# First routed layer: a part of the token tiles gathered in quarters and transposed on VectorE

## The chip, the core and the metric

The kernel runs on one core of one Trainium2 chip. The metric is the device time of one execution in microseconds; the median of several runs counts. The engines are named as in the profile: PE is TensorE (PEld its weight loads), DVE VectorE, ACT ScalarE, POOL GpSimd, SP the SyncE queue that issues plain DMAs. The granted TensorE clock averaged 0.948 of full speed in the profiled execution.

## The reference

Two layers of a gated cross-attention block with a mixture of experts behind each attention, on x of 4 x 512 tokens with 512 features, in float32. The part that matters here is the mixture of experts of the first layer:

```python
h = layernorm(x).reshape(2048, 512)
scores = sqrt(softplus(h @ gate_w.T))                 # 32 experts
_, topk_idx = top_k(scores + bias, 6)
topk_w = 1.5 * scores[topk_idx] / sum(scores[topk_idx])
pos = running count of each expert's tokens;  valid = pos < 192
xb[e, pos] = h of the token                           # 32 experts x 192 slots x 512
g = xb[e] @ w_gate[e].T ; u = xb[e] @ w_up[e].T       # 256 wide
yb[e] = (silu(g) * u) @ w_down[e].T
routed = sum over the six picks of topk_w * yb[e, pos]
x = x + tanh(g_ffn[0]) * (routed + shared expert of h)
```

Ahead of it stands the first attention (each token picks two of 64 context rows), behind it the second attention (causal, 16 heads) and a second mixture (8 experts, two picks, 352 wide, and a shared expert).

## The kernel before

**Stages.** From 0 to about 150 us the kernel runs the first attention, the norm, the gate of the first mixture and a part of its shared expert. `turn2` writes each normed tile `h` (128 tokens by 512) to `h_dram` through SP (L471) and transposes it for the gate. `gate2` computes the picks and weights; it writes the weights of each token for all 32 experts behind the token's row in `h_dram` (L552, rows of 512 + 32 floats). The running counts of the experts' tokens go to `cnt_dram` (L670). Then comes the routed loop (156 to 455 us), in which 32 experts with 192 slots each are 48 tiles of 128 slots: tiles 3q and 3q+2 hold the first and last 128 slots of the experts 2q and 2q+1, and tile 3q+1 holds the remaining 64 of both, which is called a split tile here (`parts0`).

**The routed loop** has these steps, each for one tile i:

- `find0` (L761, POOL): an indirect DMA that fetches 128 floats of counts for each slot into `found`; `count0` (L774 to L779, DVE) compares and sums them, which gives the token of each slot, `get2`. Both work on groups of four tiles (`FIND`).
- `get0` (L783, POOL): an indirect DMA that gathers the 128 tokens' rows of 544 floats into `xb`.
- `in0`: four 128x128 transposes on PE into PSUM (`ptb`, L256) and an eviction by ACT (L257) into `xbT`.
- `up0`: four matmuls of 128x512 per expert part (L801), Silu on ACT (L806), the weighted product on DVE (L808, one instruction for each expert part), which reads the slot's weight out of `xb`.
- `turn0`: two transposes (`ptj`, L817) and an eviction (L819).
- `down0`: two matmuls of 128x512 per expert part (L826), and DVE copies the result to `y` (L831), which SP stores to `y_dram` (L886).
- `weights0`: SP loads an expert's up weights (1 MB, L558) and down weights (512 KB, L559) into one of three buffers.

The order is written by hand: PE, DVE, POOL and SP carry out the instructions in program order; ahead of the loop, the order on POOL and SP is a planner's. The loop's order is

```python
for i in range(NT2):
    up0(i + 1); in0(i + 2)
    if i % 4 == 0: count0(i // 4 + 2)      # and find0 of the next group begins
    get0(i + 4); next(find, None)          # one find in each iteration
    y = down0(i)
    weights0(i + 3)
    nc.sync.dma_start(out=y_dram[...], in_=y)
    turn0(i + 1)
```

Tiles of the tag `row` (nine buffers) hold `xb`, `y` and, earlier, `h`. PSUM tags have two buffers each.

**The second mixture** (its routed tiles run from 693 us on) already has tiles that are transposed on DVE: `pair_rows4` gathers rows, SP copies them quarter by quarter so that partition 32r + s holds quarter r of the tokens, and `in4_blocks` runs one DVE instruction (L1425) that transposes every 32x32 block. The features then lie in another order over the partitions, and the weights of that layer are laid out to match (`by_32` on the host).

Of the kernel before, what the change touches and what calls it, by code (L numbers as in the profile page):

```python
# [59 lines left out]

GROUPS = [[TB * b + g for b in range(B)] for g in range(TB)]
EARLY = 2
PLACE = {t: (g, j) for g, ts in enumerate(GROUPS) for j, t in enumerate(ts)}
# [13 lines left out]
def flamingo_gated(  # L77
# [423 lines left out]
    def gate2(p):  # L501
# [47 lines left out]
        )  # L549
        hd = h_dram.rearrange("(k j p) d -> p k j d", j=TB, p=P)  # L550
        for a in range(2):
            nc.sync.dma_start(out=hd[:, :, 2 * p + a, D:], in_=wts[:, :, a, :])  # L552


# [198 lines left out]

    FIND = [range(0, 2), range(2, 4)] + [range(i, i + 4) for i in range(4, NT2, 4)]
    found = {}
# [15 lines left out]
    def count0(k):  # L771

        c, n, f = slice(FIND[k][0], FIND[k][-1] + 1), len(FIND[k]), found.pop(k)
        V.tensor_tensor(f[:, :n], f[:, :n], slots2[:, c, None].to_broadcast([P, n, P]), ALU.is_le)  # L774
        tok = tok2[:, c]
        ct = sm.tile([P, 4], F32, name=f"ct{k}", tag="ct")
        V.tensor_reduce(ct[:, :n], f[:, :n], AX.X, ALU.add)
        V.tensor_tensor(tok, tok, ct[:, :n], ALU.add)
        V.tensor_scalar(get2[:, c], tok, float(T - 1), None, ALU.min)  # L779

    def get0(i):
        rows0[i] = work.tile([P, D + E0], F32, name=f"xb{i}", tag="row", bufs=NROW)
        G.indirect_dma_start(  # L783
# [8 lines left out]
    def in0(i):  # L792
        xbTs[i] = work.tile([P, DC, P], F32, name=f"xbT{i}", tag="xnT", bufs=3)
        transposed(xbTs[i], rows0[i], f"ptb{i}")

    def up0(i):
        xbT, xb = xbTs.pop(i), rows0.pop(i)
        gu = ps.tile([P, 2 * I0], F32, name=f"gu{i}", tag="g")
        for c in range(DC):
# [7 lines left out]
        for p_, e in parts0(i):  # L807
            V.scalar_tensor_tensor(  # L808
                sg[p_, :I0], gu[p_, I0:], xb[p_, D + e : D + e + 1], sg[p_, :I0], ALU.mult, ALU.mult
            )  # L810
# [55 lines left out]
    in0(1)  # L866
    turn0(0)
    for i in range(NT2):
        if i + 1 < NT2:
            up0(i + 1)  # L870
        if i + 2 < NT2:
            in0(i + 2)
        k = i // 4 + 2
        if i % 4 == 0 and k < len(FIND):
            count0(k)
            find = find0(k + 1) if k + 1 < len(FIND) else iter(())
        if i + 4 < NT2:
            get0(i + 4)
        next(find, None)
        y = down0(i)  # L880
# [514 lines left out]
    xrs, xrTs, xqs, sgs, its = {}, {}, {}, {}, {}  # L1395
    B4 = P // 32

    def rows4(i):
# [124 lines left out]
def _host_layout(i):  # L1523
# [35 lines left out]
    for j in range(2):  # L1559
# [17 lines left out]
        "bias0": c(np.asarray(i["L0_ffn_bias"])),  # L1577
        "wgu0": k_major(beside(i["L0_ffn_w_gate"], i["L0_ffn_w_up"])),
        "wd0": k_major(t(i["L0_ffn_w_down"])),
# [35 lines left out]
```

## Time and profile before

| | us |
|---|---|
| median of 3 runs | 1103.65 (1103.22 to 1107.76) |
| the profiled execution | 1109.61 |
| its span, first to last instruction | 1107.9 |
| PE busy in the span | 1007.1 (91%) |
| DVE busy | 466.1 (42%) |
| POOL busy | 376.3 (34%) |
| ACT busy | 210.9 (19%) |
| DMA, both queues | 52.7% of 16 engines' span |

The profile is of one execution. A row of its groups gives line, engine, operation, output and inputs, shapes and count, then busy time and mean length of one, then the idle time of the engine just before these instructions and what ended it. "L256" is the helper that does all PE transposes, so the tile names (`ptb`, `pth`, ...) tell them apart. A busy PE need not be PE at its peak, as matmuls overlap: the distance between starts tells what one costs. In the timeline, consecutive instructions of one group are merged into one line with their count.

### The profile page before, as it was taken

Reading aid. Unit: us, or ns where it says so; the run is one execution under the profiler, and the core shown is the slowest. Engines: PE = TensorE matmul, PEld = TensorE weight load, DVE = VectorE, ACT = ScalarE, POOL = GpSimd, SP = SyncE. Lnnn points to the kernel's source line nnn. Section 1 sums busy time; section 2 is a strip of 40 time slices with the busy share of each in tenths; the row PEclk is TensorE's granted clock in tenths of the full one; section 3 lists DMA queues with packets and bytes.
Section 4 is the critical chain, followed back from the end, with each engine's and each line's share of the span. In section 5 each row is a group of like instructions: output and inputs, shape, how many; then the busy total and the mean of one; then the engine's idle time right before and its main releaser. Section 6 shows DMA issues by size and latency. Waiting matters only on the chain. (4 is left out here: it accounts for less than half of the span.)

```text
span 1107.9 us, 11070 instructions
## 1 busy us (share of the span) xinstructions
PE 1007.1 (91%) x3334; PEld 492.9 (44%) x3334; DVE 466.1 (42%) x1244; ACT 210.9 (19%) x461; POOL 376.3 (34%) x413
## 2 busy tenths in 40 slices
PE   5479889999999999969779896999999998999998
PEld 2134444444444444424434443655555555544443
DVE  5989946322222232357787443122222222218111
ACT  1144121222222222123343200211111111110000
POOL 2001142234332222276552562445545454310000
PEclk7679999999999999989969798999999999999999
DMA  8522047688788787765563107527453744438111
GB/s 320 234 76 77 11 125 238 222 275 283 257 294 287 253 288 248 252 204 172 145 206 115 48 5 207 184 74 238 133 163 107 248 115 145 135 117 313 38 38 38
DMA packets 88477, 191.94 MB, mean 173 GB/s; under 512 B 24638, under 2 KB 42078, under 8 KB 82016
## 3 DMA queue, kind: packets, MB, share of 16 engines
q1 hardware_dynamic: 59808, 114.59, 29.3%
q0 software_dynamic: 28608, 76.63, 23.4%
q8 instruction: 27, 0.44, 0.2%
q14 instruction: 34, 0.28, 0.1%
HBM read 206.16 MB, written 35.57 MB: 218 GB/s over the span
## 5 line engine op out<-in xcount | busy, mean ns | idle before, releaser
L801 PE MATMUL gu<-wbuf,xbT 128*128 128x512 f32 (+1 forms) x512 | 174.0, 596 | 1.7 <-ACT xbT L257 0.8
L967 POOL DMA_INDIRECT yk<-y_dram,rows_of x76 | 84.1, 1107 | 89.1 <-DMA kb<-in_kblk_dram 34.7
L783 POOL DMA_INDIRECT xb<-h_dram,get x48 | 48.1, 1002 | 165.5 <-issue 97.3
L1436 PE MATMUL pgr<-wbuf,xrT 128*128 128x352 f32 x288 | 93.2, 467 | 7.4 <-DMA wbuf<-in_wgu_dram,wrow 6.7
L1456 PE MATMUL por<-wbuf,itr 128*128 128x512 f32 (+1 forms) x216 | 98.7, 592 | 0.0
L801 PEld LDWEIGHTS gu<-wbuf,xbT 128*128 128x128 f32 (+1 forms) x512 | 63.1, 163 | 78.7 <-issue 77.3
L808 DVE SCALAR_TENSOR_TENSOR sgb<-gu,xb,sgb 128x256 f32<-128x256 f32 (+1 forms) x64 | 30.9, 483 | 157.6 <-ACT sgb L806 131.8
L1439 DVE SCALAR_TENSOR_TENSOR sgr<-pur,slots,sgr 128x352 f32<-128x352 f32 x36 | 21.0, 584 | 170.0 <-PE pur L1436 105.1
L826 PE MATMUL pob<-wbuf,itb 128*128 128x512 f32 (+1 forms) x256 | 91.2, 599 | 0.0
L1436 PE MATMUL pur<-wbuf,xrT 128*128 128x352 f32 x288 | 91.1, 459 | 0.0
L1227 PE MATMUL pg<-lnT,wbuf 128*128 128x512 f32 (+1 forms) x224 | 85.3, 560 | 0.1
L1459 POOL DMA_INDIRECT y_dram<-yr,put x36 | 36.9, 1025 | 126.5 <-DVE yr L1458 113.6
L1227 PE MATMUL pu<-lnT,wbuf 128*128 128x512 f32 (+1 forms) x224 | 79.5, 531 | 0.0
L1436 PEld LDWEIGHTS pur<-wbuf,xrT 128*128 128x128 f32 x288 | 54.7, 190 | 30.5
L1436 PEld LDWEIGHTS pgr<-wbuf,xrT 128*128 128x128 f32 x288 | 52.7, 193 | 32.1 <-issue 4.5
L1243 PE MATMUL po<-wbuf,it 128*128 128x512 f32 x128 | 61.2, 612 | 3.0 <-DVE x L1253 3.0
L1456 PEld LDWEIGHTS por<-wbuf,itr 128*128 128x128 f32 (+1 forms) x216 | 41.0, 190 | 41.9 <-issue 34.9
L761 POOL DMA_INDIRECT found<-cnt_dram,look x48 | 48.7, 1014 | 25.9 <-issue 14.0
L1227 PEld LDWEIGHTS pg<-lnT,wbuf 128*128 128x128 f32 (+1 forms) x224 | 35.6, 183 | 43.8 <-issue 42.0
L1227 PEld LDWEIGHTS pu<-lnT,wbuf 128*128 128x128 f32 (+1 forms) x224 | 35.0, 175 | 40.8 <-issue 38.1
L831 DVE COPY y<-pob 128x512 f32<-128x512 f32 x48 | 33.2, 692 | 45.3 <-PE pob L826 32.0
L1458 DVE TENSOR_TENSOR yr<-por,half_db 128x512 f32<-128x512 f32 x36 | 24.9, 692 | 57.5 <-PE por L1456 51.2
(398 smaller groups left out, 1279.2 us busy)
## 6 DMA issues: line engine op xcount, KB each, us to landing
wbuf<-in_wgu_dram SPq DMA_DIRECT2D x32, 1024.0 KB
wbuf<-in_wd_dram SPq DMA_DIRECT2D x32, 512.0 KB
y_dram<-y SPq DMA_DIRECT2D x48, 256.0 KB
q<-rp SPq DMA_DIRECT2D x256, 32.0 KB
y<-y_dram SPq DMA_DIRECT2D x32, 256.0 KB
lnT<-in_xT_dram SPq DMA_DIRECT2D x4, 1024.0 KB
x<-in_x_dram SPq DMA_DIRECT2D x16, 256.0 KB
h_dram<-h SPq DMA_DIRECT2D x16, 256.0 KB
```

The costliest lines, as they stand in the source:

```text
L761: G.indirect_dma_start(out=found[k][:, j, :], out_offset=None, in_=cnt_dram[:, :], in_offset=bass.IndirectOffsetOnAxis(ap=look2[:, i : i + ...
L783: G.indirect_dma_start(out=rows0[i], out_offset=None, in_=h_dram[:, :], in_offset=bass.IndirectOffsetOnAxis(ap=get2[:, i : i + 1], axis=0) ...
L801: PE.matmul(gu[p_, :], lhsT=xbT[:, c, p_], rhs=weights[e][0][:, c, :], start=(c == 0), stop=(c == DC - 1),)
L808: V.scalar_tensor_tensor(sg[p_, :I0], gu[p_, I0:], xb[p_, D + e : D + e + 1], sg[p_, :I0], ALU.mult, ALU.mult)
L826: PE.matmul(po[p_, :], lhsT=it[:, ic, p_], rhs=weights[e][1][:, ic, :], start=(ic == 0), stop=(ic == I0 // P - 1),)
L831: V.tensor_copy(y, po)
L967: G.indirect_dma_start(out=yk, out_offset=None, in_=y_dram[:, :], in_offset=bass.IndirectOffsetOnAxis(ap=rows_of[:, t, k : k + 1], axis=0) ...
L1227: PE.matmul(p_[m, :n], lhsT=wgu[:, a, c, i], rhs=lnT[g][:, c, k], start=(c == 0), stop=(c == DC - 1))
L1243: PE.matmul(po, lhsT=it[:, ic, k * P : (k + 1) * P], rhs=wd[:, ic, :] if ic < 2 else wd2, start=(ic == 0), stop=(ic == 2),)
L1436: PE.matmul(p_, lhsT=xbT[:, c, :], rhs=wgu[:, a, c, :], start=(c == 0), stop=(c == DC - 1))
L1456: PE.matmul(po, lhsT=it[:ni, ic, :], rhs=wd[:ni, ic, :], start=(ic == 0), stop=(ic == 2))
L1459: d = G.indirect_dma_start(out=y4_dram[:, :], out_offset=bass.IndirectOffsetOnAxis(ap=put4[:, i : i + 1], axis=0), in_=yr, in_offset=None, ...
```

## The change

Of the 48 tiles, 18 are handled in another way: those of every second pair of experts from the sixth on (tiles 15 to 17, 21 to 23, ..., 45 to 47; `hops`). For these

- `get0` issues five indirect DMAs instead of one: four gather 128 rows of 128 floats (quarters of a token's row, out of a second copy of h, `hq_dram`), so that partition 32r + s of block a holds quarter r of the token of slot 32a + s; the fifth gathers the 32 weights of each slot's token from `w_dram`;
- `in0` is one DVE transpose of 32x32 blocks from SBUF to SBUF, with no PE transposes and no eviction by ACT;
- the row numbers of the quarters come from one small matmul (`quarters0`: 128x128 `same_b` by 12 columns, PE) and a conversion on DVE; `count0` has two small instructions more;
- the up and gate weights of those experts are laid out on the host with `by_32`.

Finds and counts go by groups of three tiles from tile 12 on, in an order written out by tables; the gathers of the 18 tiles are issued five iterations ahead, the others four as before. In the stage ahead of the loop, `turn2` stores each h a second time (`hq_dram`), `gate2` stores the weights a second time (`w_dram`), and POOL makes the constants `quarter`, `in_quarter` and `same_b`.

```diff
+HOP = 15
...
+    hq_dram = dram.tile([T, D], F32, name="hq_dram")
+    w_dram = dram.tile([T, E0], F32, name="w_dram")
...
+    B4 = P // 32
+    quarter = sm12.tile([P, 1], F32, name="quarter")
+    in_quarter = sm12.tile([P, B4], F32, name="in_quarter")
+    same_b = sm12.tile([P, P], F32, name="same_b")
+    G.memset(in_quarter, 0.0)
+    G.memset(same_b, 0.0)
+    for a in range(B4):
+        G.memset(quarter[32 * a : 32 * a + 32, :], float(a))
+        G.memset(in_quarter[32 * a : 32 * a + 32, a : a + 1], 1.0)
+        for r in range(B4):
+            G.tensor_tensor(
+                same_b[:, 32 * r : 32 * r + 32], same_b[:, 32 * r : 32 * r + 32], ident[:, 32 * a : 32 * a + 32], ALU.add
+            )
+    spread = sm12.tile([P, 3 * B4], F32, name="spread")
...
             nc.sync.dma_start(out=h_dram[t * P : (t + 1) * P, :D], in_=h)
+            nc.sync.dma_start(out=hq_dram[t * P : (t + 1) * P, :], in_=h)
...
-        hd = h_dram.rearrange("(k j p) d -> p k j d", j=TB, p=P)
+        hd, wd_ = [d.rearrange("(k j p) d -> p k j d", j=TB, p=P) for d in (h_dram, w_dram)]
         for a in range(2):
             nc.sync.dma_start(out=hd[:, :, 2 * p + a, D:], in_=wts[:, :, a, :])
+            nc.sync.dma_start(out=wd_[:, :, 2 * p + a, :], in_=wts[:, :, a, :])
...
-    FIND = [range(0, 2), range(2, 4)] + [range(i, i + 4) for i in range(4, NT2, 4)]
+    FIND = [range(0, 2), range(2, 4), range(4, 8), range(8, 12)]
+    for i in range(HOP, NT2, 6):
+        FIND += [range(i - 3, i), range(i, i + 3)]
+    hops = [i for t in range(HOP, NT2, 6) for i in range(t, t + 3)]
+    wcols, quarter_idx = {}, {}
...
         V.tensor_scalar(get2[:, c], tok, float(T - 1), None, ALU.min)
+        if FIND[k][0] in hops:
+            V.tensor_scalar(tok, tok, float(T - 1), None, ALU.min)
+            V.tensor_tensor(
+                spread[:, : 4 * n].rearrange("p (j a) -> p j a", a=B4),
+                tok[:, :, None].to_broadcast([P, n, B4]), in_quarter[:, None, :].to_broadcast([P, n, B4]), ALU.mult,
+            )
+
+    def quarters0(k):
+
+        n = len(FIND[k])
+        pi = ps.tile([P, 4 * n], F32, name=f"pi{k}", tag="u")
+        PE.matmul(pi, lhsT=same_b, rhs=spread[:, : 4 * n], start=True, stop=True)
+        idx = sm12.tile([P, 4 * n], I32, name=f"qi{k}", tag="qi", bufs=2)
+        V.tensor_scalar(idx, pi, 4.0, quarter, ALU.mult, ALU.add)
+        wc = sm12.tile([P, n, E0], F32, name=f"wc{k}", tag="wc", bufs=2)
+        for j, i in enumerate(FIND[k]):
+            quarter_idx[i], wcols[i] = idx[:, 4 * j : 4 * j + 4], wc[:, j, :]
 
     def get0(i):
+        if i in hops:
+            rows0[i] = work.tile([P, B4, P], F32, name=f"xq{i}", tag="row", bufs=NROW)
+            hq = hq_dram.rearrange("t (r d) -> (t r) d", d=P)
+            for dst, src, idx, n in [
+                *((rows0[i][:, a, :], hq, quarter_idx[i][:, a : a + 1], 4 * T) for a in range(B4)),
+                (wcols[i], w_dram, get2[:, i : i + 1], T),
+            ]:
+                G.indirect_dma_start(
+                    out=dst, out_offset=None, in_=src[:, :],
+                    in_offset=bass.IndirectOffsetOnAxis(ap=idx, axis=0), bounds_check=n - 1, oob_is_err=False,
+                )
+            return
...
         xbTs[i] = work.tile([P, DC, P], F32, name=f"xbT{i}", tag="xnT", bufs=3)
+        if i in hops:
+            V.transpose(
+                out=xbTs[i].rearrange("p c (a t) -> p a c t", a=B4),
+                in_=rows0[i].rearrange("p a (c t) -> p a c t", t=32),
+            )
+            return
         transposed(xbTs[i], rows0[i], f"ptb{i}")
...
+    counts_at, gets_at, finds_at = {0: 2, 4: 3}, {}, {i: [3] for i in range(4)}
+    for i in range(4, NT2):
+        gets_at.setdefault(i - (5 if i in hops else 4), []).append(i)
+    for k, ts in enumerate(FIND[4:], 4):
+        counts_at[ts[0] - (6 if k % 2 else 5)] = k
+        for j in range(3):
+            at = 4 + j // 2 if k == 4 else ts[0] - 9 + j
+            finds_at.setdefault(at, []).append(k)
+    finds = {k: find0(k) for k in range(3, len(FIND))}
     for i in range(NT2):
...
-        k = i // 4 + 2
-        if i % 4 == 0 and k < len(FIND):
-            count0(k)
-            find = find0(k + 1) if k + 1 < len(FIND) else iter(())
-        if i + 4 < NT2:
-            get0(i + 4)
-        next(find, None)
+        if i - 1 in counts_at and FIND[counts_at[i - 1]][0] in hops:
+            quarters0(counts_at[i - 1])
+        if i in counts_at:
+            count0(counts_at[i])
+        for j in gets_at.get(i, ()):
+            get0(j)
+        for k in finds_at.get(i, ()):
+            next(finds[k])
```

More of the change, by code (lines that the diff above doesn't have):

```diff
@@ L797, in up0 @@
         xbT, xb = xbTs.pop(i), rows0.pop(i)
+        wc = wcols.pop(i) if i in hops else xb[:, D:]
         gu = ps.tile([P, 2 * I0], F32, name=f"gu{i}", tag="g")
@@ L808, in up0 @@
             V.scalar_tensor_tensor(
-                sg[p_, :I0], gu[p_, I0:], xb[p_, D + e : D + e + 1], sg[p_, :I0], ALU.mult, ALU.mult
+                sg[p_, :I0], gu[p_, I0:], wc[p_, e : e + 1], sg[p_, :I0], ALU.mult, ALU.mult
             )
@@ L1395, in flamingo_gated @@
     xrs, xrTs, xqs, sgs, its = {}, {}, {}, {}, {}
-    B4 = P // 32
     def rows4(i):
@@ L1577, in _host_layout @@
         "bias0": c(np.asarray(i["L0_ffn_bias"])),
-        "wgu0": k_major(beside(i["L0_ffn_w_gate"], i["L0_ffn_w_up"])),
+        "wgu0": np.stack([
+            (by_32 if q >= HOP // 3 and q % 2 == HOP // 3 % 2 else k_major)(beside(i["L0_ffn_w_gate"][e], i["L0_ffn_w_up"][e]))
+            for q, e in ((e // 2, e) for e in range(E0))
+        ]),
         "wd0": k_major(t(i["L0_ffn_w_down"])),
```

## The prediction

> **What bounds the kernel now.** I read the page's groups first, to see which engine is without idle time in the first layer's routed loop (48 tiles, 156 to 455 us), then the windows of the loop, and then its timeline for two tiles.
>
> ```profile
> L801 PE MATMUL gu<-wbuf,xbT 128*128 128x512 f32 (+1 forms) x512 | 174.0, 596 | 1.7 <-ACT xbT L257 0.8
> L783 POOL DMA_INDIRECT xb<-h_dram,get x48 | 48.1, 1002 | 165.5 <-issue 97.3
> ```
> TensorE waits 1.7 us in all before the 512 up matmuls, while GpSimd sat idle 165.5 us before its 48 gathers.
>
> ```profile
> 300.00:318.00 18.00, 18.00 (x68) 7.82 (x67) 4.68 (x8) 4.03 (x9) 4.20 (x5) 1.00 0.90 307
> 318.00:336.00 18.00, 18.00 (x68) 7.83 (x67) 5.05 (x11) 4.03 (x9) 7.98 (x8) 1.00 0.87 288
> ```
> Columns: length, then busy time of PE, PEld, DVE, ACT and POOL, clock, DMA share, GB/s. TensorE is busy 18.00 of 18 us at full clock: the loop runs at TensorE's pace. The second thing to see is 0.90 and 0.87: the DMA engines are nearly full. From 246 to 444 us the windows average 0.80.
>
> ```profile
> L256 PE MATMUL ptb<-ident,xb 128*128 128x128 f32 x192 | 29.8, 278 | 2.3 <-DMA xb<-h_dram,get 2.3
> ...
> L1425 DVE STREAM_TRANSPOSE xrT<-q 128x512 f32<-128x512 f32 x32 | 22.4, 701 | 0.0
> ```
> The first row is what the change takes away from 18 tiles, the second, from the second layer, is what it puts there: an identical instruction.
>
> ```profile
> 291.67 0.60 PE L256 MATMUL ptb<-ident,xb 128*128 128x128 f32 x4
> ...
> 292.11 1.88 PE L826 MATMUL pob<-wbuf,itb 128*128 128x512 f32 x4
> ...
> 295.30 1.00 POOL L783 DMA_INDIRECT xb<-h_dram,get  x1 [15.14 <-issue]
> ...
> 296.60 1.00 POOL L761 DMA_INDIRECT found<-cnt_dram,look  x1 [0.30 <-issue]
> ...
> 297.73 0.66 PE L256 MATMUL ptb<-ident,xb 128*128 128x128 f32 x4
> ...
> 298.22 1.88 PE L826 MATMUL pob<-wbuf,itb 128*128 128x512 f32 x4
> 298.29 0.98 DVE L808 SCALAR_TENSOR_TENSOR sgb<-gu,xb,sgb 64x256 f32<-64x256 f32 x2 [3.14 <-ACT sgb L806]
> ...
> 299.94 0.38 PE L817 MATMUL ptj<-ident,sgb 128*128 128x128 f32 x2
> ...
> 300.16 3.60 PE L801 MATMUL gu<-wbuf,xbT 128*128 128x512 f32 x8
> ...
> 300.86 0.33 SPq L886 DMA_DIRECT2D y_dram<-y  x1
> ...
> 301.28 0.50 SPq L558 DMA_DIRECT2D wbuf<-in_wgu_dram  x1
> ...
> 312.17 3.65 PE L801 MATMUL gu<-wbuf,xbT 128*64 128x512 f32 x16
> ```
> Matmul starts give the pace: a tile takes 297.73 - 291.67 = 6.06 us (6.02 over many). The four transposes hold TensorE from 291.67 to 292.11, 0.44 us, and in their neighbours 0.49 and 0.53. GpSimd issues one indirect DMA per 1.30 us. A split tile's weights (L558, 301.28) are issued behind the store of a finished tile (300.86); by the trace's packet records they land at 309.7, and their tile starts at 312.17: 2.4 us of slack. Two later ones have 3.9 and 3.3.
>
> The way into the loop:
>
> ```profile
> 136.00 0.91 SPq L552 DMA_DIRECT2D h_dram<-wts  x2
> ...
> 137.01 0.46 SPq L558 DMA_DIRECT2D wbuf<-in_wgu_dram  x1
> ...
> 140.79 0.36 SPq L670 DMA_DIRECT2D cnt_dram<-counts  x1
> ...
> 144.10 1.71 POOL L761 DMA_INDIRECT found<-cnt_dram,look  x1 [11.60 <-DVE chain L704]
> ```
> ```profile
> 154.64 0.66 PE L256 MATMUL ptb<-ident,xb 128*128 128x128 f32 x4 [2.32 <-DMA xb<-h_dram,get]
> ```
> These stores run in one row: packets of wts 136.90 to 138.49, of wgu to 141.77, of the counts to 142.84, and only then can the finds start. TensorE waits for the end of this chain, 2.32 us.
>
> **The change, part by part.**
>
> *Removed from TensorE:* 18 of 48 tiles lose their four transposes: 18 x 0.49 (mean of 0.44, 0.49, 0.53) = 8.8 us, all on the path. The Trainium skill (TensorE: Matmul & The Clock Gate, Part 4) gives about 275 ns for one transpose in a kernel's context, and the row above says 278; by that 72 of them would be 20 us. But 278 ns is one's length, pipeline included, and the next work starts 0.44 to 0.53 us after four. I take the starts: 8.8. The 18 ScalarE evictions (0.59 each) bring nothing; ScalarE is busy 4 of 18 us.
>
> *Added to TensorE:* six index matmuls (`same_b` by 12 columns). Nearest is the second layer's 128x8 one, L1028: four of them are 8 records in 1.87 us, first starts 0.22 apart, two records each, so 0.44. Six: 2.6 us; if the loads hide, half: 1.3.
>
> *VectorE's transposes:* 18 x 0.70 us. VectorE has room (5 of 18 us busy), but it is in order: the transpose of tile i+2 stands behind the weighting of tile i+1 (L808) and must end before up0(i+2). For a whole tile L808 ends about 1.05 us after up0; plus 0.70 that is just in time for the 1.94 to 2.15 us of down and turn. Behind a split tile there are two L808 (0.98): 298.29 + 0.98 + 0.70 = 299.97, while TensorE without transposes would be ready at 297.73 + 1.72 + 0.22 = 299.67. With semaphores 0.35 us, six times: 2.1 us (0 to 3.5). That is where the cover by ptb goes. Two small instructions per count and one for the index (0.17 to 0.2 each) lie in VectorE's idle time.
>
> *GpSimd:* a converted tile issues five gathers for one. Six tiles then take 6 finds + 3 + 15 = 24 DMAs x 1.30 = 31.2 us of about 35; before it was 15.6 of 36. Not the bound on average, but no longer ahead. Let S be the start of the iteration five before a converted group. Index matmul and conversion end near S + 4.7, so the first quarter starts at S + 4.9. Behind it the other group's third find is number 11 (S + 19.2) and the next converted group's third find number 20 (S + 30.9). A DMA lands 3.1 to 8.4 us after issue in the loop (packet records; 5.7 in the mean). The counts that need them come up on VectorE about 5.2 us into the third and 5.7 us into the fifth iteration after S, with 5.85 us each at S + 22.8 and S + 35.0. Finds land at 25 and 36.6: VectorE waits some 2 us at each, with `y`'s copy, the next L808 and transpose queued behind it. What it costs TensorE through late L808s and index matmuls: most is absorbed in two `o` buffers; I take 0.4 us for each of five pairs, 2.0 us (0 to 8).
>
> *SP and the weights:* the count at S + 35 delays the copy and store of tile b, the first of its group; directly behind that store in SP's queue is wgu of the next split tile. A 2 us wait plus the count's 1.7 us puts the store some 3 to 4 us late against 2.4 to 3.9 us of slack, from which the faster tiles take another 1. Excess about 0.6 us in five pairs: 3.0 us (0 to 10).
>
> *DMA load:* a converted tile moves 256 + 16 KB instead of 272. The old gather is 64 packets of 207 ns. For four gathers of 128 rows of 512 B the nearest row is the find, same shape: 16 packets each, median 182 but mean 490 ns. So 11.6 to 31.4 us of packet time against 13.2: per engine -0.1 to +1.1 us per tile, plus about 0.1 for the 128 B rows. Finds read few, shared rows; spread rows should be near the low end. I take nothing and keep +1.1 for the range.
>
> *A port rule against the change:* the Trainium skill (SBUF — State Buffer, the box on DVE blocking a SWDGE DMA) says that GpSimd cannot write descriptors during a two-port VectorE instruction. Were the transpose one, 0.70 us of lockout per tile would be 2.1 of GpSimd's 4 us of slack per pair. In the second layer GpSimd's gathers (L1262) keep 1.007 us where L1425 runs, so I count none.
>
> *Before the loop:* two more stores of 64 KB in 128 B rows (w_dram) stand in SP's queue ahead of wgu and the counts. The same bytes took 136.90 to 138.49, so the finds start 1.6 us later, and TensorE's 2.32 us wait grows by that: 1.6 us (0 if SP's planner puts the counts ahead). The 16 hq stores (4 MB) fall at 62 to 105 us, DMA share 0.2: hidden; without that cover about 14 us. GpSimd's 26 small set-up instructions (0.1 to 0.3 each) lie in its idle time from 7.6 to 88 us. By the reordered weights of six expert pairs no byte changes.
>
> **Sum:** -8.8 + 2.6 + 2.1 + 2.0 + 3.0 + 1.6 = +2.5 us, on the profiled execution's 1109.61 (span 1107.9, 1.7 around it) about 1112. That execution lies 6 us over the median of the runs; the difference carried over gives 1103.65 + 2.5 = 1106. Against this kernel a measurement can tell about 0.5%, 5.5 us, from no change.
>
> **The rivals.**
>
> 1. *Break-even*, as summed: 1106, own range 1099 to 1109. Chance 0.47.
>
> 2. *Late weights.* DMA share is already 0.9, and wgu waits in SP behind a store behind a count. It decides once the count's wait passes about 2.4 us, or packets near 490 ns stretch a 4 us weight load by a tenth. Then both split tiles of a pair are late, 11 times by 1.2 us: +13 instead of +3, in all +12.5: 1116. Against: TensorE shows no weight wait today. Chance 0.27.
>
> 3. *GpSimd becomes the bound.* At a pitch of 1.5 instead of 1.30 us, 24 DMAs are 36 us, over the 35 of six tiles; the chain find, count, index, gather then sets the pace, about 1.5 us per pair beyond the sum: +10, 1114; with longer landings +20. Against: every kind of indirect DMA here takes 1.0 to 1.1 us. Chance 0.18.
>
> 4. *All waits absorbed.* Index matmul at 1.3, transpose stall 1.0, no late count or weight: -8.8 + 1.3 + 1.0 + 0.8 = -5.7: 1098. For: VectorE has two thirds free. Against: finds' landing times as measured. Chance 0.08.
>
> **Numbers.** Predicted 1106. From 1098 (rival 4) to 1122 (rivals 2 and 3 without their far ends). Faster 0.08, same 0.47, slower 0.27 + 0.18 = 0.45.
>
> **What would show it.** Right: ptb at 120 instead of 192; 18 STREAM_TRANSPOSE of 0.70; GpSimd near nine tenths in converted stretches; VectorE waiting on DMA before L774's instruction inside the loop, none today; up0 waiting 0.3 us on transposes behind split tiles; first find 1.6 us later. Wrong: idle before the up matmuls above 12 us and released by wbuf (rival 2); a GpSimd pitch above 1.4 or VectorE's transposes waiting on quarters (rival 3); six tiles in under 35.2 us (rival 4).

## The result, and the profile after

In the first measurement the changed kernel took 1164.91 us (median of 4 runs, 1160.02 to 1167.72) against 1105.70 for the kernel before (4 runs, 1103.22 to 1108.89): a ratio of 1.053, 95% interval 1.0486 to 1.0574. Two later sets of runs of the same two kernels, on chips that the results number 4 and 8, gave this:

| set | kernel before | changed kernel | ratio, 95% interval |
|---|---|---|---|
| first | 1105.70 | 1164.91 | 1.053, 1.0486 to 1.0574 |
| chip 4 | 1101.80 | 1108.52 | 1.0053, 1.0033 to 1.0074 |
| chip 8 | 1109.98 | 1161.82 | 1.0491, 1.0442 to 1.0539 |

(The chip of the first set is not on record.) The ratios are over fast runs and differ a little from those of the medians; front_only, in the table of the experiments, had two slow runs in twenty, which its median counts. The same program costs 0.5% on one chip and 5% on another. So there are two questions: what the change costs wherever it runs, and what adds some 50 us on some chips. The first set's profile shows the second. Its groups, for the whole program:

```profile
L864 PE MATMUL gu<-wbuf,xbT 128*128 128x512 f32 (+1 forms) x512 | 190.9, 632 | 16.0 <-issue 13.0
L839 POOL DMA_INDIRECT xb<-h_dram,get x30 | 30.1, 1004 | 75.0 <-issue 36.5
L833 POOL DMA_INDIRECT xq<-hq_dram,qi x72 | 71.7, 996 | 76.3 <-DVE qi L820 56.2
```
These answer to the up matmuls and the row gathers shown of before. TensorE now waits 16.0 us ahead of the up matmuls, 13.0 of it for "issue", that is for nothing that the profile shows. GpSimd's gathers are still 1.00 us each, and it still has idle time: 75.0 and 76.3 us.

The two windows of the loop (columns as before: length, busy PE, PEld, DVE, ACT, POOL, clock, DMA share, GB/s):

```profile
300.00:318.00 18.00, 13.31 (x28) 5.15 (x29) 3.81 (x9) 1.51 (x4) 9.03 (x10) 0.83 0.51 161
318.00:336.00 18.00, 17.77 (x65) 7.66 (x64) 7.37 (x17) 3.19 (x8) 6.48 (x7) 1.00 0.77 268
```
In the first window TensorE is busy 13.31 of 18 us at a clock of 0.83, and the DMA engines fell from 0.90 to 0.51, so they are not what is short. From the first transpose of the loop to its last down matmul it is 352.0 us; it was 298.5 (156.93 to 508.9, and 154.64 to 453.2, in the traces).

The clock is a part of the loss. In the loop of before it is granted in full throughout; here it is halved in eight stretches, 43.5 us in all, and each of them begins during a wait of TensorE's of over 1 us or within 2 us after one. The stretch inside the first window, and the time behind it:

```profile
299.40:302.80 3.40, 3.02 (x4) 1.47 (x5) 0.00 (x0) 0.33 (x1) 2.65 (x3) 0.50 0.31 85
302.80:306.00 3.20, 2.18 (x5) 0.62 (x4) 0.69 (x1) 0.00 (x0) 2.43 (x3) 1.00 0.26 86
```
A 128x512 matmul that starts in such a stretch lasts 1.03 us in the mean, the others 0.60. Over the loop TensorE is idle 41.1 us where it was 2.7, and busy 310.8 us where it was 295.9, although 72 transposes are gone. The waits come first and the slower clock comes on top.

The timeline tells what TensorE waits for. From the up matmuls of tile 19 to the silu of tile 20, while GpSimd gathers the quarters of tiles 21 to 23:

```profile
290.67 3.65 PE L864 MATMUL gu<-wbuf,xbT 128*64 128x512 f32 x16
291.28 1.00 POOL L833 DMA_INDIRECT xq<-hq_dram,qi  x1 [0.30 <-issue]
292.58 0.99 POOL L833 DMA_INDIRECT xq<-hq_dram,qi  x1 [0.30 <-issue]
...
294.26 0.65 PE L275 MATMUL ptb<-ident,xb 128*128 128x128 f32 x4
294.75 1.88 PE L889 MATMUL pob<-wbuf,itb 128*128 128x512 f32 x4
...
296.31 0.38 ACT L869 ACTIVATE sgb<-gu 128x256 f32<-128x256 f32 x1 [4.82 <-PE ptb L275]
...
297.85 0.41 PE L880 MATMUL ptj<-ident,sgb 128*128 128x128 f32 x2 [1.22 <-DVE sgb L871]
...
299.15 0.59 ACT L276 COPY xbT<-ptb 128x512 f32<-128x512 f32 x1 [2.46 <-issue]
299.78 5.19 PE L864 MATMUL gu<-wbuf,xbT 128*128 128x512 f32 x8 [1.53 <-issue]
...
304.04 0.69 DVE L894 COPY y<-pob 128x512 f32<-128x512 f32 x1 [6.33 <-issue]
...
306.19 0.37 ACT L882 COPY itb<-ptj 128x256 f32<-128x256 f32 x1 [6.46 <-PE gu L864]
...
310.42 0.38 ACT L869 ACTIVATE sgb<-gu 128x256 f32<-128x256 f32 x1 [3.86 <-remote]
```
Read each follower against the matmuls that it follows. up0 ends at 294.32 by its record, its silu starts at 296.31. The four transposes end at 294.91, their eviction starts at 299.15. The down matmuls end at 296.63, `y`'s copy starts at 304.04: 7.41 us behind. Right ahead of these two, ACT had been idle for 2.46 us and DVE for 6.33 us. The other way there is no such delay: the eviction of xbT ends at 299.74 and the next up matmul starts at 299.78; of TensorE's waits in this loop that ACT or DVE ended, none lasted more than 0.15 us past the end of their instruction. Only what TensorE tells the others comes late, and where TensorE needs their answer the lag comes back to it as a wait: 1.22 us ahead of the turn, 1.53 us ahead of the up matmuls.

On chip 4 the same stage looks like this:

```profile
284.53 0.99 POOL L833 DMA_INDIRECT xq<-hq_dram,qi  x1 [0.30 <-issue]
284.68 0.66 PE L275 MATMUL ptb<-ident,xb 128*128 128x128 f32 x4
284.82 0.38 ACT L869 ACTIVATE sgb<-gu 128x256 f32<-128x256 f32 x1 [2.91 <-PE gu L864]
285.18 1.88 PE L889 MATMUL pob<-wbuf,itb 128*128 128x512 f32 x4
...
285.38 0.58 ACT L276 COPY xbT<-ptb 128x512 f32<-128x512 f32 x1 [0.17 <-PE ptb L275]
285.83 1.00 POOL L833 DMA_INDIRECT xq<-hq_dram,qi  x1 [0.31 <-issue]
...
287.10 0.69 DVE L894 COPY y<-pob 128x512 f32<-128x512 f32 x1 [0.88 <-PE pob L889]
```
The eviction starts 0.04 us after the transposes' end and `y`'s copy 0.04 us after the down matmuls' end, with GpSimd issuing its gathers every 1.30 us there too.

The Trainium skill (Perfetto Trace Analysis, the part on the Tensor Engine instruction) says that a matmul's recorded end is estimated from its size, and that its semaphore update is pushed later, once PSUM has acknowledged the writes. This trace fits that: the end is 294.91, and the follower moves at 299.15. So a late follower may mean that the results came late into PSUM or that the news of them did, and no run here tells the two apart. I count a follower as late when it starts over 1 us after that end and its engine had been idle for 1 us or more just before it. In the routed loop the first set's trace has 31 of them, up to 9.6 us; chip 8's 31, up to 10.9 us; chip 4's none.

### The profile page after: what moved, and what is told of

It is laid out like the page before. It is cut to its first block, busy times and chain, and to the rows that moved or that the text cites. A ratio compares the mean times of both kernels' runs of the same rounds, so it can differ in the third digit from the quotient of the medians.

```text
span 1164.7 us, 11224 instructions
## 1 busy us (share of the span) xinstructions
PE 1019.9 (88%) x3274; PEld 490.5 (42%) x3274; DVE 482.5 (41%) x1292; ACT 200.2 (17%) x443; POOL 450.7 (39%) x511
## 5 line engine op out<-in xcount | busy, mean ns | idle before, releaser
L864 PE MATMUL gu<-wbuf,xbT 128*128 128x512 f32 (+1 forms) x512 | 190.9, 632 | 16.0 <-issue 13.0
L864 PEld LDWEIGHTS gu<-wbuf,xbT 128*128 128x128 f32 (+1 forms) x512 | 69.1, 175 | 106.1 <-issue 100.2
L833 POOL DMA_INDIRECT xq<-hq_dram,qi x72 | 71.7, 996 | 76.3 <-DVE qi L820 56.2
L871 DVE SCALAR_TENSOR_TENSOR sgb<-gu,xb,sgb 128x256 f32<-128x256 f32 (+1 forms) x40 | 19.3, 483 | 126.4 <-issue 67.4
L839 POOL DMA_INDIRECT xb<-h_dram,get x30 | 30.1, 1004 | 75.0 <-issue 36.5
L1301 PEld LDWEIGHTS pg<-lnT,wbuf 128*128 128x128 f32 (+1 forms) x224 | 35.4, 182 | 43.5 <-issue 41.7
```

What stands on the lines that cost most here:

```text
L833: G.indirect_dma_start(out=dst, out_offset=None, in_=src[:, :], in_offset=bass.IndirectOffsetOnAxis(ap=idx, axis=0), bounds_check=n - 1, o ...
L839: G.indirect_dma_start(out=rows0[i], out_offset=None, in_=h_dram[:, :], in_offset=bass.IndirectOffsetOnAxis(ap=get2[:, i : i + 1], axis=0) ...
L864: PE.matmul(gu[p_, :], lhsT=xbT[:, c, p_], rhs=weights[e][0][:, c, :], start=(c == 0), stop=(c == DC - 1),)
L1301: PE.matmul(p_[m, :n], lhsT=wgu[:, a, c, i], rhs=lnT[g][:, c, k], start=(c == 0), stop=(c == DC - 1))
```

## The experiments

Theories at the start: (A) TensorE's results come late while GpSimd issues indirect DMAs densely; (B) the new chain of index, gather, transpose and matmul holds TensorE; (C) the added transfers take the DMA engines from the weights. D to G were added as runs came in; their expectations say what they are. Each set ran on one chip, and every ratio is against the kernel before on that chip. "Late" counts followers in the routed loop as above.

| run | chip | us | ratio, 95% interval | late |
|---|---|---|---|---|
| burst | 12 | 1147.17 | 1.042, 1.0383 to 1.0457 | 0 |
| burst_small | 12 | 1135.85 | 1.0292, 1.0252 to 1.0331 | 0 |
| even | 12 | 1133.24 | 1.0266, 1.023 to 1.0302 | 0 |
| whole | 12 | 1098.36 | 0.9974, 0.9958 to 0.999 | 0 |
| again | 4 | 1108.52 | 1.0053, 1.0033 to 1.0074 | 0 |
| nowc | 4 | 1100.87 | 0.9987, 0.997 to 1.0005 | 0 |
| pe | 4 | 1114.09 | 1.0111, 1.0077 to 1.0145 | 0 |
| early | 4 | 1107.05 | 1.0046, 1.0032 to 1.0059 | 0 |
| again2 | 8 | 1161.82 | 1.0491, 1.0442 to 1.0539 | 31 |
| before2 | 8 | 1110.15 | one run | 6 |
| front_only | 8 | 1113.75 | 1.0034, 1.0011 to 1.0058 | 5 |
| whole2 | 5 | 1107.21 | 0.9991, 0.9956 to 1.0026 | 3 |
| burst2 | 5 | 1184.26 | 1.0697, 1.061 to 1.0784 | 36 |
| ops | 5 | 1125.15 | 1.0163, 1.0087 to 1.024 | 5 |
| via | 5 | 1146.89 | 1.0359, 1.028 to 1.0437 | 3 |
| via2 | 11 | 1101.47 | 0.9983, 0.9962 to 1.0004 | 0 |
| nowc2 | 11 | 1100.38 | 0.9978, 0.9953 to 1.0002 | 0 |
| even2 | 11 | 1132.56 | 1.0269, 1.0214 to 1.0325 | 0 |

**Spare gathers in the kernel before, chip 12.** burst, burst_small and even add this to the loop of before, with the scratch tiles for it:

```
+    def spare0(n):
+        for _ in range(n):
+            j = next(extra)
+            G.indirect_dma_start(
+                out=dump[j % 8], out_offset=None, in_=cnt_dram[:, :],
+                in_offset=bass.IndirectOffsetOnAxis(ap=look2[:, j % NT2 : j % NT2 + 1], axis=0), ...
...
         if i + 4 < NT2:
             get0(i + 4)
+        if i in range(10, 43, 6) or i in range(11, 43, 6) or i in range(12, 43, 6):
+            spare0(4)
         next(find, None)
```
burst_small takes rows of 8 columns from the same table; even calls `spare0(2)` for every i from 9 to 44.

> The kernel before, with four spare gathers of 512 bytes a row (72 in all, into scratch that nothing reads) issued by GpSimd in the iterations in which the changed kernel gathers its quarters. Nothing else of the change is in it. Theory A (TensorE's results come late while GpSimd issues indirect DMAs back to back, whoever needs them): 1145 to 1165 us, six tiles at 44 to 47 us, and the followers of TensorE in ACT and DVE 2 to 9 us behind in those iterations. Theory B (the new chain of index, gather, transpose and matmul holds TensorE): 1103 to 1110, since that chain is not here. Theory C (the added transfers take the DMA engines from the weights): 1110 to 1125, with the weights landing late.

> As the run with 72 spare gathers in bursts, but each brings 32 bytes a row in place of 512: as many GpSimd instructions and as many rows, a sixteenth of the bytes. Theory A: the same loss as with 512 bytes, 1145 to 1165. Theory C: 1104 to 1108. Theory B: 1103 to 1108.

> The kernel before, with the same 72 spare gathers of 512 bytes a row, but two in each of 36 iterations in place of four in each of 18. Theory A as a matter of long runs of gathers: TensorE's lags mostly gone, 1104 to 1115. Theory A as a matter of the number of gathers: 1145 to 1165 as with the bursts. Theory C: 1110 to 1125, as many bytes. Theory B: 1103 to 1110.

Only burst's 1147 lies in a forecast range, that of theory A; 1135.85 and 1133.24 lie in none. And theory A's mechanism is not there: not one follower is late. The rows of the burst trace, in the loop, show what was:

```profile
L257 PE MATMUL ptb<-ident,xb 128*128 128x128 f32 x188 | 30.7, 288 | 18.7 <-DMA xb<-h_dram,get 18.7
...
L776 DVE TENSOR_TENSOR found<-found,slot_no 128x512 f32<-128x512 f32 x11 | 7.6, 689 | 24.3 <-DMA found<-cnt_dram,look 24.3
```
TensorE waits 18.7 us for rows, and VectorE 24.3 us for finds with `y`'s copies queued behind: both stand in GpSimd's queue behind the spare gathers. A time within the forecast was no proof of the reason. burst_small, at a sixteenth of the bytes, has 0.7 of burst's loss (2.92 of 4.2%), which leaves theory C at most the rest.

**One gather of the whole row, chip 12.** The changed kernel, with

```
-            rows0[i] = work.tile([P, B4, P], F32, name=f"xq{i}", tag="row", bufs=NROW)
-            hq = hq_dram.rearrange("t (r d) -> (t r) d", d=P)
-            for dst, src, idx, n in [
-                *((rows0[i][:, a, :], hq, quarter_idx[i][:, a : a + 1], 4 * T) for a in range(B4)),
-                (wcols[i], w_dram, get2[:, i : i + 1], T),
-            ]:
+            rows0[i] = work.tile([P, D + E0], F32, name=f"xb{i}", tag="row", bufs=NROW)
+            for dst, src, idx, n in [(rows0[i], h_dram, get2[:, i : i + 1], T)]:
...
-                in_=rows0[i].rearrange("p a (c t) -> p a c t", t=32),
+                in_=rows0[i][:, :D].rearrange("p (a c t) -> p a c t", a=B4, t=32),
...
-        wc = wcols.pop(i) if i in hops else xb[:, D:]
+        wc = xb[:, D:]
```

> The changed kernel, but each converted tile takes its rows and its expert weights by one gather of the whole row, as the kernel before does, and VectorE transposes the 32x32 blocks of that: the values in the converted tiles are mixed up, the work of TensorE, VectorE and ScalarE is that of the changed kernel. The index matmuls, the stores of the copy and the weight table stay. Theory A: 1098 to 1110, no lags. Theory B: 1150 to 1165, as the chain is still there. Theory C: 1098 to 1110.

1098.36: VectorE's transposes, the index matmuls and the front stay, and with GpSimd's four further gathers gone the change is a gain of 0.26%. Theory B falls here. The changed kernel itself was not run on this chip, so for a chip on which it loses 5% the same version had to be run once more (whole2, below).

**The changed kernel and three variants, chip 4.** again is the changed kernel. nowc leaves the gather of `w_dram` out and uses `ones[:, :E0]`. pe calls `transposed(xbTs[i], rows0[i]..., ...)` for converted tiles too. early is

```
-        counts_at[ts[0] - (6 if k % 2 else 5)] = k
+        ahead = 2 if k > 5 else 0
+        counts_at[ts[0] - (6 if k % 2 else 5) - ahead] = k
...
-            at = 4 + j // 2 if k == 4 else ts[0] - 9 + j
+            at = 4 + j // 2 if k == 4 else ts[0] - 9 + j - ahead
```
with three found tiles of its own.

> The changed kernel once more, beside its variants. In its first trace TensorE's results reached ACT and DVE 2 to 9 us after the recorded ends of its matmuls; in the four runs with spare or whole gathers they did not, though GpSimd issued as densely. Theory A (results held back while GpSimd issues back to back): the lags are there again, 1155 to 1167 us. Theory D (a loop through GpSimd's queue: finds, count, index matmul, 15 gathers, transposes, and the next finds behind them, longer than six tiles of TensorE): 1155 to 1167 us, and a trace with fewer lags shows TensorE idle in front of matmuls that wait for a gather, a count or a transpose.

> The changed kernel without the fifth gather of each converted tile (its expert weights; a column of ones stands in for them): three of 24 gathers in six tiles fall away. Theory D: each gather of the loop costs its 1.30 us pitch, so six tiles fall by about 3.9 us and the kernel by 20 to 25: 1135 to 1145. Theory A (a matter of long runs of gathers): 15 gathers in a row in place of 18, a few us less, 1150 to 1160. Theory B (the dependent chain alone): 1155 to 1166, the chain being as long.

> The changed kernel with its five gathers a tile, but TensorE turns the converted tiles as before and ScalarE evicts them, in place of VectorE's transposes; the values in those tiles are mixed up. Theories A and D: the gathers are all there, so the loss stays: 1155 to 1175. Theory B in the form that VectorE's transposes hold the matmuls: 1105 to 1120.

> The changed kernel with the finds and counts of the groups from tile 18 on two tiles earlier (in found tiles of their own, three of them); the gathers of the rows stay where they are, as many and as dense. Theory D: the count and the index matmul no longer end the wait in front of the quarter gathers, GpSimd's idle time of some 16 us in six tiles falls, and six tiles come to 36 to 41 us: 1105 to 1135. Theory A: as dense as before, 1150 to 1166. Theory B: the same chain with more slack, 1110 to 1140.

All four expectations started from 1160, but on this chip the changed kernel is at 1108.52. pe's and early's times lie in a range all the same (theory B's 1105 to 1120, theory D's 1105 to 1135), by luck: the loss that was to go had not been there. The runs can still be compared with each other: without the fifth gather the kernel is 7.7 us faster (1108.52 - 1100.87, for 18 gathers); with TensorE's transposes in place of VectorE's it is 5.6 us slower (1114.09 - 1108.52, uncertain by some 4); earlier counts change 1.5 us, within the intervals. The rows of again, 150 to 520 us, the counts' row 156 to 475 us:

```profile
L864 PE MATMUL gu<-wbuf,xbT 128*128 128x512 f32 (+1 forms) x512 | 178.9, 610 | 3.2 <-DVE xbT L851 2.5 <-ACT xbT L276 0.7
...
L275 PE MATMUL ptb<-ident,xb 128*128 128x128 f32 x120 | 18.6, 278 | 4.2 <-DMA xb<-h_dram,get 4.2
...
L851 DVE STREAM_TRANSPOSE xbT<-xq 128x512 f32<-128x512 f32 x18 | 12.7, 704 | 0.2
...
L799 DVE TENSOR_TENSOR found<-found,slot_no 128x384 f32<-128x384 f32 (+1 forms) x14 | 8.1, 576 | 32.9 <-issue 19.0 <-DMA found<-cnt_dram,look 13.9
...
L818 PE MATMUL pi<-spread,same_b 128*128 128x12 f32 x12 | 2.0, 243 | 3.9 <-DVE spread L807 3.9
```
This is what the change costs without lags: TensorE waits 2.5 us for VectorE's transposes and 3.9 us ahead of the index matmuls; VectorE waits 32.9 us ahead of the counts in the loop, where the kernel before had 0.1:

```profile
L774 DVE TENSOR_TENSOR found<-found,slot_no 128x512 f32<-128x512 f32 x11 | 7.5, 685 | 0.1
```
In nowc this wait is 1.8 us, and no index matmul waits. So on this chip the cost goes with the fifth gather; that it does so by letting the finds come sooner in GpSimd's queue is the likely reading, but was not tested apart.

**The changed kernel again, and the front alone, chip 8.** front_only is the kernel before with the stores of `hq_dram` and `w_dram` and GpSimd's constants.

> The changed kernel a third time, perhaps on another chip. Theory E (the loss of the first measurement belongs to the chip or the state that it ran in, where TensorE's semaphore updates reached the other engines late, and not to the change alone): either 1105 to 1112 us with followers 0.1 us behind TensorE, as in the second measurement, or 1155 to 1168 us with followers 2 to 9 us behind, as in the first; nothing between. Theory A (the change brings the lags with it): the second should have shown them, and this one should too: 1155 to 1168.

> The kernel before, for a trace beside that of the changed kernel on the same chip. Theory E: if the changed kernel is at 1105 to 1112 there, this trace has no follower over 1 us behind TensorE in the routed loop, where the first trace of before had three (1.1 to 2.1 us), and about 16,000 to 17,000 recorded semaphore updates in place of 10,771; if it is at 1155 or more, it has the lags of the first trace. 1098 to 1108 us in either case.

> The kernel before with only the front of the change: the second store of the normalised rows, the two stores of the weight table per pass, GpSimd's constants; the loop is that of before. By the prediction's steps (late stores ahead of the counts 1.6 us, GpSimd's constants hidden) 1102 to 1105, a ratio of 1.001 to 1.002. If the +0.5% of the second measurement lies in the front: 1107 to 1109, a ratio of 1.005 to 1.006.

Theory E holds so far: 1161.82 with 31 late followers, nothing between. The kernel before has late followers here too, six up to 2.2 us (four in the first set's trace, not the three that the expectation gives), and at 1110.15 it lies a little above its forecast. The front alone costs 0.34%, 3.8 us on 1109.98, between the two forecasts of 0.1 to 0.2% and 0.5 to 0.6%. That the program alone does not bring the lags is shown; what in the change calls them up was left to the next set.

**Gathers or transposes, on a chip that lags: chip 5.** whole2 and burst2 are the kernels from above. ops is burst with `G.memset(blank, 0.0)` in place of the spare gather. via is the version with one gather, no second copy of the rows, no weight table and no index matmuls; its core is

```
+    def out0(i):
+        nc.sync.dma_start(out=xs_dram[hops.index(i)], in_=rows0[i][:, :D])
+
+    def back0(i):
+        xqs0[i] = sm12.tile([P, B4, P], F32, name=f"xq{i}", tag="xq", bufs=2)
+        src = xs_dram[hops.index(i)].rearrange("(a t) (r d) -> r t a d", t=32, d=P)
+        for r in range(DC):
+            nc.sync.dma_start(out=xqs0[i][32 * r : 32 * r + 32], in_=src[r])
...
         nc.sync.dma_start(out=y_dram[i * P : (i + 1) * P, :], in_=y)
+        if i + 4 in hops:
+            out0(i + 4)
+        if i + 3 in hops:
+            back0(i + 3)
```

> The changed kernel with one whole-row gather in place of five for each converted tile (values in those tiles mixed up, work of the other engines unchanged), once more. Theory F (on some chips, or in some state of theirs, TensorE's semaphore updates reach the other engines late while GpSimd issues gathers densely; the change raises that density): on such a chip the lags of 2 to 9 us and nearly the whole loss are gone, ratio 0.995 to 1.01; on the other kind 0.997 as before. Theory G (on such a chip it is the transposes, or the chain through them, that brings the lags): 1.03 to 1.05 there.

> The kernel before with 72 spare gathers in bursts, once more. Theory F: on a chip of the first kind (followers 2 to 9 us behind TensorE with the changed kernel) lags of several us stand in the bursts here too, on top of GpSimd's queue, 1150 to 1180 us; on the other kind 1147 as before, without lags. Theory G: no lags on either kind, 1140 to 1155.

> The kernel before with four memsets of a 128x1024 tile (some 1.0 us each, estimated from the 529 ns of the 128x512 one) in the iterations in which the changed kernel gathers quarters, 72 in all, nothing else: GpSimd as long busy, no DMA added. If the lags come of GpSimd being busy: lags on a chip of the first kind, 1130 to 1170. If they come of its DMAs: none there, and the kernel loses only what its in-order queue delays finds and gathers: 1115 to 1145 on either kind.

> A version that computes the same as both kernels: each converted tile takes one whole-row gather, SP stores it to DRAM and reads it back in four DMAs with the quarters in place, and VectorE transposes the blocks; no index matmuls, no second copy of the rows, no weight table. GpSimd issues as many gathers as in the kernel before. Theory F: no lags on either kind of chip, ratio 0.993 to 1.003 (what the run with whole gathers gave, less the front that falls away, plus 90 SP DMAs in front of stores and weights). If SP's added DMAs hold the weights up: 1.01 to 1.03.

burst2, the kernel before plus gathers that nothing reads, has 36 late followers, up to 10.6 us, and loses 7.0% where burst lost 4.2% (1184.26, just above theory F's 1150 to 1180). Its timeline at one of them:

```profile
296.28 3.70 PE L814 MATMUL gu<-wbuf,xbT 128*128 128x512 f32 x8
...
308.35 0.38 ACT L819 ACTIVATE sgb<-gu 128x256 f32<-128x256 f32 x1 [9.42 <-remote]
```
The up matmuls end at 299.98 and their silu starts 8.4 us later. whole2 has all of the transposes and three late followers of at most 1.9 us, and takes no longer than before. So on such a chip the lags come with the density of GpSimd's gathers, not with the transposes: theory F, against G. ops keeps GpSimd busy for as long (72 memsets of 0.96 us) and has five late followers, up to 1.9 us, no more than the kernel before on chip 8; its 1125.15 lies in the range forecast for a queue that only delays finds and gathers. Being busy is not enough, a run of indirect DMAs is what it takes.

The nine traces with late followers say how long a run. GpSimd's indirect DMAs come in unbroken runs, one per 1.30 us, and every late follower in the routed loops stands at one. No matmul that ended in the first 8 us of a run (about six gathers) has a late follower, and none starts late more than 3.7 us behind the start of the run's last gather. Every run of 12 or more has late followers, of the runs of 7 to 9 some have, and no shorter run has any. The changed kernel's long runs are of 15 and 19, those of the kernel before of 8 at most. On chip 4 the changed kernel has a run of 24 (236.38 to 266.29 us) without a late follower.

via has no more lags than the kernel before, but loses 3.6%, more than either forecast: it is SP's order, as this row of its VectorE in the loop tells, followed by the same row of via2:

```profile
L821 DVE STREAM_TRANSPOSE xbT<-xq 128x512 f32<-128x512 f32 x18 | 12.8, 711 | 34.3 <-DMA xq<-xs_dram 34.1
```
```profile
L821 DVE STREAM_TRANSPOSE xbT<-xq 128x512 f32<-128x512 f32 x18 | 12.7, 705 | 3.0 <-DMA xq<-xs_dram 2.8 <-issue 0.2
```

**The moved version, and two repeats: chip 11.** via2 puts the calls of `out0` and `back0` ahead of `weights0(i + 3)`, and so ahead of the wait for `y`'s copy.

> The version with one gather, a store and four loads on SP, with these SP DMAs put ahead of the weights and the store of y in each iteration, so some 5 us earlier (in the first placing VectorE's transposes waited 34.1 us for the loads, and TensorE 24.5 us for the transposes). If those waits were its loss: 1.00 to 1.01 of before. If SP's added DMAs delay weights and stores: 1.02 to 1.04.

> The changed kernel without the fifth gather of each converted tile (a column of ones stands in for its expert weights), once more. Theory F on a chip of the lagging kind: 15 in place of 18 gathers in a burst, so the lags stay but shrink: 1.02 to 1.04 of before. On the other kind 0.997 to 1.001, as before.

> The kernel before with 72 spare gathers, two in each of 36 iterations, once more. Theory F on a chip of the lagging kind: runs of 16 gathers at four in 6 us (the group of four finds and its rows), so followers 1 to 8 us behind here too, and 1.04 to 1.07; if only bursts of six a tile bring lags: 1.027 as on the other kind.

This chip does not lag, so the repeats only repeat: 0.9978 and 1.0269. nowc and even were not measured on a chip that lags. via2 is level with before: 0.9983, an interval that holds 1, with the long wait for the loads gone. It was not run on a chip that lags, so no version here is shown to beat the kernel before.

## Why the prediction was wrong

It forecast 1106 with a range of 1098 to 1122; the first set gave 1164.91. On chip 4 the changed kernel is at 1108.52, 6.7 us over before against a forecast of 2.5. By its own steps:

- *Removed transposes, -8.8, and VectorE's stall, +2.1.* Together -6.7; pe shows 5.6, uncertain by some 4. The stall itself is in again's waits: 2.5 us in all, as 11 waits of at most 0.3 us and not six of 0.35. Right in size. The count of 120 `ptb` and 18 transposes of 0.70 us came as forecast.
- *Index matmuls, +2.6.* They hold TensorE 0.22 to 0.29 us each, 1.6 in all, but it also waits 3.9 us for `spread` ahead of them, which the sum did not have: VectorE writes it behind the late counts.
- *Late counts, +2.0.* VectorE's wait was longer than the assumed 2 us each: 1.4 to 4.8 us at ten counts, 32.9 us ahead of the counts of the loop where the kernel before has 0.1. TensorE's share of it stayed small on chip 4: it waits 3.6 us ahead of the turns, behind late weighting (0.9 before), beside the 3.9 above.
- *Late weights, +3.0.* Not there: in again, and in the first set's trace, no wait of TensorE's in the loop ended with `wbuf`. Rival 2 falls.
- *The front, +1.6.* The first find came at 145.99 and TensorE's wait for it grew from 2.32 to 5.08 us:

```profile
145.99 1.27 POOL L786 DMA_INDIRECT found<-cnt_dram,look  x1 [13.13 <-DMA cnt_dram<-counts]
```
```profile
156.93 1.11 PE L275 MATMUL ptb<-ident,xb 128*128 128x128 f32 x4 [5.08 <-DMA xb<-h_dram,get]
```
  The find is 1.9 us later, close to the forecast, but the wait is not the whole cost. On chip 8 TensorE's wait ahead of the first transposes grew from 1.75 us (before2) to 4.09 (front_only), and the first up matmuls behind it took 5.19 us where they had taken 3.70. Their rows in before2 and front_only:

```profile
156.30 3.70 PE L801 MATMUL gu<-wbuf,xbT 128*128 128x512 f32 x8 [0.68 <-ACT xbT L257]
```
```profile
158.98 5.19 PE L819 MATMUL gu<-wbuf,xbT 128*128 128x512 f32 x8 [0.68 <-ACT xbT L273]
```
  In front_only the granted clock is 0.50 from 158.6 to 162.0 us, in before2 1.00 there. So 2.3 + 1.5 = 3.8 us, which is what the whole front measured (interval 1.2 to 6.4). The sum had no term for a clock that falls behind a wait.

- *The rest of chip 4.* In again's loop the clock is halved once more, for 3.4 us from 300.9 on, 1.7 us lost. An estimate from these rows, the forecast's -8.8 and the stall's 2.5, 1.6 and 3.9 for the index matmuls, 2.7 more ahead of the turns, 3.8 for the front and 1.7 for the clock, gives 7.4 us, near the 6.7 measured. That the forecast's 2.5 came as near as it did is partly luck: late weights were put too high, index matmuls and front too low.
- *GpSimd's four further gathers per tile.* **This is the step that failed.** "Not the bound on average, but no longer ahead" weighed them as time in GpSimd's queue only, and rival 3 let them cost more in one way, a longer pitch. The pitch stayed at 1.30 us and GpSimd had idle time: from 236 to 332 us of again it is busy 0.55 to 0.76 of each of four stretches, not near nine tenths. Against one whole gather they cost 0.8% on chips without lags (1.0053 on chip 4 against 0.9974 on chip 12, some 9 us on 1102). On chips that lag they cost 5.0% (1.0491 on chip 8 against 0.9991 on chip 5, 55 us on 1110), because TensorE's results reach ACT and DVE late while they are issued, TensorE waits for the answers, and its clock is halved behind the waits. These comparisons are across chips; on no chip were both versions run. Not one term of the sum or of the rivals had a path from GpSimd's DMAs to TensorE's completions.

The trace of before showed that path at a smaller size, in a stretch of its timeline with a run of gathers that I had not read:

```profile
275.24 1.00 POOL L783 DMA_INDIRECT xb<-h_dram,get  x1 [0.30 <-PE ptj L817]
...
276.54 1.00 POOL L761 DMA_INDIRECT found<-cnt_dram,look  x1 [0.30 <-issue]
277.85 1.00 POOL L783 DMA_INDIRECT xb<-h_dram,get  x1 [0.30 <-issue]
278.61 0.66 PE L256 MATMUL ptb<-ident,xb 128*128 128x128 f32 x4
279.10 1.88 PE L826 MATMUL pob<-wbuf,itb 128*128 128x512 f32 x4
279.15 1.00 POOL L761 DMA_INDIRECT found<-cnt_dram,look  x1 [0.30 <-issue]
...
281.39 0.59 ACT L257 COPY xbT<-ptb 128x512 f32<-128x512 f32 x1 [1.76 <-PE ptj L817]
281.45 0.69 DVE L831 COPY y<-pob 128x512 f32<-128x512 f32 x1 [0.80 <-PE ptj L817]
282.03 1.55 PE L801 MATMUL gu<-wbuf,xbT 128*128 128x512 f32 x3 [0.83 <-ACT xbT L257]
```
The transposes end at 279.26, their eviction starts at 281.39, after an idle wait that is put down to a `ptj` of another tile, and TensorE loses 0.83 us. A wait that the profile puts down to a later instruction than the one that feeds the waiting one, or to "issue", was the sign. It stands at the end of a run of eight indirect DMAs (270.02 to 279.15 us), and the change makes runs of 19 (283.48 to 306.87 us, one per 1.30).

Why some chips lag is open. The first set and chips 8 and 5 did, chips 12, 4 and 11 did not; each chip was seen in one set only, so the chip, its state and its neighbours' work are not told apart. Open, too, is what in a gather does it: burst_small's few bytes were only seen on a chip without lags.

## What to carry to other kernels

Before work is moved to GpSimd as more indirect DMAs, look at its densest stretch in the profile and compare, one by one, the end of each matmul with the start of the ACT or DVE instruction that reads it; over 1 us with an idle follower is a warning that more gathers there may cost TensorE time, whatever GpSimd's own idle time says. Count how many indirect DMAs follow each other without a break, not only bytes or queue share, and try one gather per tile with the rearrangement done elsewhere. Where TensorE comes to wait, look at its clock in the microseconds behind the wait as well. A ratio measured on one chip may be that chip's: where a result has a mechanism that one trace shows and another does not, measure on a second before believing either.

## What the hardware did that I had not expected

- With GpSimd issuing indirect DMAs 1.30 us apart, TensorE's followers started up to 10.9 us after the recorded end of its matmuls on some chips and, when idle, as a rule 0.04 to 0.1 us after it on others (at most 0.4), with the same instructions. ScalarE's and VectorE's results were not late: in the same lagging traces TensorE moved 0.05 to 0.15 us behind them.
- In the lagging trace of before three updates of TensorE's semaphore come in a bunch: those of the transposes, of the down matmuls and of the turn, which end by their records at 279.26, 280.98 and 281.20, are recorded at 281.37, 281.43 and 281.47. The down matmuls take 1.88 us and cannot have run in the 0.06 us after the transposes, so it is their completion, the write or the news of it, that was held, or an earlier instruction's in front of it. Of the changed kernel's 625 TensorE instructions that update it, the first set's trace holds 528 updates and chip 8's 526; chip 4's holds 624. All semaphores together, the traces of the first set and of chips 8 and 5 hold 10,335 to 12,267 updates, also those with few late followers (whole2 11,407), and those of chips 12, 4 and 11 16,196 to 17,458: it is a mark of the chip or its state, not of the lags. Whether updates were merged or the recording lost them, and whether the recording itself holds TensorE's updates up, no run here shows.
- TensorE's granted clock was halved for 3.4 to 10.2 us at a time, always beginning in or shortly behind a wait of over 1 us: 43.5 us of the first set's loop, 10.2 us of chip 4's, none in the loops of the two traces of the kernel before, one of which has a wait of 2.32 us.
- Where chips lag, the kernel before is little slower: its medians are 1105.70, 1109.98 and 1107.37 there, and 1102.27, 1101.80 and 1102.10 elsewhere, 3 to 8 us more. Whether late followers are all of that is not shown.
